# SS2D scan layer: dt*x copied into PSUM by ScalarE instead of TensorE, and products with C made for two tiles at a time

## The chip, the cores and the metric

The kernel runs on one core of a Trainium2 chip. The time is the device time of one execution in microseconds, from the first to the last instruction of that core. Before the change it is 18467.62 us, the median of three runs (18457.31 to 18490.28). The execution that the profiler recorded has a span of 18479.8 us.

## What is computed

Four layers work on a batch of eight images of 56 x 56 pixels with 128 channels. Layers 0, 2 and 3 are deformable convolutions and are not touched. Layer 1 is a visual state-space block ("SS2D"): after a projection, a 3 x 3 convolution and SiLU, each image is read as a sequence of L = 3136 positions in K = 4 directions, and each direction runs a linear recurrence with 256 channels and N = 16 states for each channel. This is the part of the reference that the change bears on:

```python
dt = jax.nn.softplus(dt + dt_projs_b[None, :, :, None])
A = -jnp.exp(A_logs).reshape(K, Di, N)

def step(h, t):
    dt_t, u_t, B_t, C_t = t
    h = h * jnp.exp(dt_t[..., None] * A) + (dt_t * u_t)[..., None] * B_t[:, :, None, :]
    y = jnp.einsum('bkdn,bkn->bkd', h, C_t)
    return (h, y)
```

Each channel and state has a decay exp(dt * A), an input dt * x * B, a recurrence over the positions, and an output that is the sum over the 16 states of h * C.

## The kernel before

**Tiles.** A direction of an image is cut into four chunks of 784 positions (SC). Eight images, four directions and four chunks make 128 steps, which run one after the other. Within a step there are 256 x 16 rows of (channel, state); one tile holds 32 channels with 4 states each on 128 partitions, by 784 positions. So a step has 32 tiles: eight channel groups (`cg`) by four state groups (`sg`), with `sg` running fastest. "Group" below means the four tiles of one `cg`.

**What a tile does.** `decay` (L1346) has ScalarE write dA = exp(dt * A) into PSUM (two buffers). `inputs` makes u = dt * x * B: for the first three tiles of a group VectorE multiplies (L1356) dt * x, which it reads in PSUM, with B; for the fourth GpSimd does it (L1352, tile `up`, one buffer), from SBUF. The dt * x of a group gets into PSUM through `spread` (L1340): TensorE multiplies it with the identity, two matmuls for each group, which the trace shows as four records, into the tile `dtu`. `dtu` has one buffer of two banks, so the next group's can be written only when VectorE has made the third u of this group. Then VectorE runs the recurrence (L1449, a scan) into `h` (three buffers), ScalarE copies its last column to `st` for the next chunk (L1452, a tiny instruction), GpSimd multiplies h with C into `hc` (L1454, six buffers), and TensorE sums the states by matmuls with a 0/1 matrix into `acc` (`add_sums`, L1378). `close_sums` (L1389) has ScalarE copy `acc` out once every eight tiles, and `open_sums` (L1370) starts the next one.

**Around it.** `prepare` (L1241 on) makes dt, dt * x, B and C of the next step in pieces, with matmuls into the one `misc` bank, ScalarE activations (L1265 to L1269) and two GpSimd operations on `dd` (L1271, L1273) for each half of the channels. The input stage of the next image and the output stage of finished chunks run in the background, a piece every tile or two. The SyncE queue issues all transfers: `fetch_dt` (L1291) for a group, two groups ahead, and `fetch_row` (L1284) for B and C of the next step, four rows of each, in five buffers each.

**What sets the order.** The whole layer is written out without a loop. A scheduler puts the instructions of each engine into one fixed order when the program is built; on the chip each engine takes its instructions in that order, and an instruction that has to wait holds up all that stand behind it on its engine. `add_sums` is traced under `issue_after(self.last_spread)`, which puts its matmuls behind the last `spread` on TensorE.

Of the kernel before, what the change touches and what calls it, by code (L numbers as in the profile page):

```python
# [41 lines left out]
F32 = mybir.dt.float32  # L42
# [76 lines left out]
SC, SR = 784, 14  # L119
NSC = L // SC  # L120
SH = SC // 2
# [11 lines left out]
TC, TS = 32, 4  # L133
NCG, NSG = DI // TC, NST // TS
# [855 lines left out]
class Vss:  # L990
# [286 lines left out]

    def fetch_row(self, s, x, sg):

        name = "bc"[x]  # L1280
        t = s[name, sg] = self.work.tile([128, SC], F32, name=name, tag=name, bufs=NSG + 1)
        r = s["rows"]
        src = bass.AP(tensor=r.tensor, offset=r.offset + TS * sg * 2 * SC + x * SC, ap=[[0, TC], [2 * SC, TS], [1, SC]])
        self.nc.sync.dma_start(out=t, in_=src)  # L1284
# [15 lines left out]
    def scans(self):  # L1300
        nc, w = self.nc, self.w
        self.gates, self.sums = {}, {}
        self.y = self.img.tile([128, NCH, L], F32, name="y", tag="y")
        steps = [(i, k, c) for i in range(self.images) for k in (1, 3, 0, 2) for c in (range(NSC) if k < 2 else reversed(range(NSC)))]

        order = [(cg, sg) for cg in range(NCG) for sg in range(NSG)]
# [5 lines left out]
        state = [dict() for _ in steps]  # L1312
# [9 lines left out]
        def advance(count):  # L1322
            for _ in range(count):
                while tasks:
                    try:
                        next(tasks[0])
                        break
                    except StopIteration:
                        tasks.popleft()

        def on_pool(t):

            return order[t][1] == NSG - 1

        def spread(at, t):

            s, (cg, sg) = state[at], order[t]
            ps = s["dtu", cg] = self.pdtu.tile([128, 2, 512], F32, name="dtu", tag="dtu")
            for b in range(2):
                last = nc.tensor.matmul(ps[:, b, :SH], lhsT=self.net.ident, rhs=s["dt", cg][:, 1, SH * b : SH * (b + 1)], start=True, stop=True)  # L1340
            self.last_spread = last.ins

        def decay(at, t):
            (i, k, c), s, (cg, sg) = steps[at], state[at], order[t]
            da = s["dA", t] = self.pda.tile([128, 1024], F32, name="dA", tag="dA")
            nc.scalar.activation(da[:, :SC], s["dt", cg][:, 0], AF.Exp, scale=w["A"][:, k, NSG * cg + sg : NSG * cg + sg + 1])  # L1346

        def inputs(at, t):
            s, (cg, sg) = state[at], order[t]
            if on_pool(t):  # L1350
                u = self.work.tile([128, SC], F32, name="up", tag="up", bufs=1)
                nc.gpsimd.tensor_mul(u, s["dt", cg][:, 1], s["b", sg])  # L1352
            else:
                u = self.work.tile([128, SC], F32, name="u", tag="u", bufs=2)
                halves = [v.rearrange("p (x e) -> p x e", x=2) for v in (u, s["b", sg])]
                nc.vector.tensor_mul(halves[0], s["dtu", cg][:, :, :SH], halves[1])  # L1356
            s["u", t] = u
# [13 lines left out]

        def add_sums(at, group):
            acc = state[at]["acc"]
            with self.tc.issue_after(self.last_spread):
                for (cg, sg), hc in group:
                    for b in range(2):
                        r = 64 * b + TC * (cg % 2)
                        nc.tensor.matmul(acc[r : r + TC, :SH], lhsT=w["sum"], rhs=hc[:, SH * b : SH * (b + 1)], start=False, stop=sg == NSG - 1)  # L1378

        def close_sums(at, t):  # L1380
            (i, k, c), acc, (h, r) = steps[at], state[at]["acc"], place(t)
# [12 lines left out]
            if t == NT - 1:  # L1394
                state[at] = None
                if k == 2:
                    tasks.extend(self.output_stage(i, e) for e in (2 * c + 1, 2 * c))

        spread(*units[0])
        decay(*units[0])  # L1400
        inputs(*units[0])
        st = ready = None
        group, late = [], deque()
        zeros = self.zeros()
        for now, (at, t) in enumerate(units):
            (i, k, c), s, (cg, sg) = steps[at], state[at], order[t]
            forward = k < 2
            if t == 0:
                if at % NSC == 0:
                    st = self.prep.tile([128, NT], F32, name="st", tag="st", bufs=2)  # L1410
                    nc.gpsimd.memset(st, 0.0)
                if at % (NDIR * NSC) == 0 and i + 1 < self.images:
                    tasks.append(self.input_stage(i + 1))
                ready = iter(())
                if at + 1 < len(steps):
                    if steps[at + 1][0] > i:
                        self.load_xb(i + 1)
                    ready = self.prepare(state[at + 1], *steps[at + 1][1:])
            if t % (2 * NSG) == 0:
                late.append((now + 5, open_sums, (at, t)))  # L1420
            while late and late[0][0] <= now:
                _, do, args = late.popleft()
                do(*args)
            if t % 2 == 0:
                next(ready, None)

            if sg == 1:
                to = divmod(NCG * at + cg + 2, NCG)
                if to[0] < len(steps):
                    self.fetch_dt(state[to[0]], to[1])  # L1430
            if t in (3, 19):
                next(zeros, None)

            for x, when in enumerate(((25, 28, 29, 30), (26, 29, 30, 31))):
                if t in when and at + 1 < len(steps):
                    self.fetch_row(state[at + 1], x, when.index(t))
            if now + 1 < len(units):
                decay(*units[now + 1])
                if not on_pool(units[now + 1][1]):
                    inputs(*units[now + 1])  # L1440

                if sg == NSG - 3 and now + 3 < len(units):
                    spread(*units[now + 3])
            if now + 2 < len(units) and on_pool(units[now + 2][1]):
                inputs(*units[now + 2])
            hh = self.work.tile([128, SC], F32, name="h", tag="h", bufs=3)
            step = 1 if forward else -1
            u, dA = s.pop(("u", t)), s.pop(("dA", t))
            nc.vector.tensor_tensor_scan(hh[:, ::step], dA[:, :SC][:, ::step], u[:, ::step], st[:, t : t + 1], ALU.mult, ALU.add)  # L1449
            if c != (NSC - 1 if forward else 0):  # L1450
                last = SC - 1 if forward else 0
                nc.scalar.copy(st[:, t : t + 1], hh[:, last : last + 1])  # L1452
            hc = self.work.tile([128, SC], F32, name="hc", tag="hc", bufs=6)
            nc.gpsimd.tensor_mul(hc, hh, s["c", sg])  # L1454
            group.append((order[t], hc))
            if t % 2:
                late.append((now + 3, add_sums, (at, group)))
                group = []
                if t % (2 * NSG) == 2 * NSG - 1:
                    late.append((now + 5, close_sums, (at, t)))  # L1460
            if t % 2 or t % 4 == 0 or (i == self.images - 1 and k == 2):
                advance(1)
# [81 lines left out]
```

## Time and profile before

The scan layer lies between 2366 us and 13800 us of the span: the first scan starts at 2365.9 us, the last ends just before 13801 us. The other layers lie before and after it. The table is of the profiled execution.

| | before |
|---|---|
| median of three runs | 18467.62 us |
| span of the profiled execution | 18479.8 us |
| the scan layer, from 2366 to 13800 us | 11434 us |
| one step (a 128th of it) | 89.3 us |
| VectorE busy in the scan layer | 10264 us |
| GpSimd busy in the scan layer | 10454 us |
| ScalarE busy in the scan layer | 7052 us |
| TensorE (matmul) busy in the scan layer | 8638 us |

A row of the profile's groups of instructions names the line, the engine, the operation, output and inputs, then how often it ran, its total busy time in us and the mean of one in ns, and then the idle time of its engine just before it, with what ended that idle time. A list of waits names for one engine which instruction waited for which, with the sum, the count and the longest in us. A line of the timeline has the start and the length in us; an "x4" is four records run together, and the bracket is the idle time before them.

### The profile page before, as it was taken

How to read it: one execution, taken by the hardware profiler on the slowest of the kernel's cores; microseconds unless marked ns; L12 is line 12 of the kernel's file. 1: busy time of each engine (PE TensorE's matmuls, PEld its weight loads, DVE VectorE, ACT ScalarE, POOL GpSimd, SP SyncE). 2: the span in 40 equal slices, each digit the busy share in tenths (PEclk: the TensorE clock that was granted, in tenths of full speed). 3: DMA queues.
4: the chain of work that ended last, by engine and by line, in shares of the span. 5: the costliest groups of instructions: out<-in, count | busy, mean ns of one | idle time of the engine just before them, and what ended most of it. 6: DMA issues, size and time to landing. Idle time of an engine off the chain costs nothing. (4 is left out here: it accounts for less than half of the span.)

```text
span 18479.8 us, 257190 instructions
## 1 busy us (share of the span) xinstructions
PE 13780.6 (75%) x89795; PEld 6844.2 (37%) x89795; DVE 15510.8 (84%) x18797; ACT 11145.4 (60%) x20690; POOL 11801.5 (64%) x6462
## 2 busy tenths in 40 slices
PE   5777787678678778678778768767665888577777
PEld 4555422222222222222222222222224666455555
DVE  8888379988988988988988898898985887688886
ACT  4666565566566566566566656656554666456666
POOL 2221089998998998998998998899981111222221
PEclk7878888889889889889888888888886888677777
DMA  7777444444443444344343443443433777577777
GB/s 215 205 210 200 122 158 160 162 158 148 142 149 137 146 147 140 140 150 139 140 150 136 143 152 135 143 150 136 147 122 110 196 198 198 143 204 204 201 204 175
DMA packets 1341779, 2961.90 MB, mean 160 GB/s; under 512 B 91168, under 2 KB 892132, under 8 KB 1325836
## 3 DMA queue, kind: packets, MB, share of 16 engines
q1 hardware_dynamic: 1340460, 2945.21, 51.4%
q8 instruction: 718, 11.76, 0.3%
q14 instruction: 601, 4.92, 0.1%
HBM read 2243.88 MB, written 866.92 MB: 168 GB/s over the span
## 5 line engine op out<-in xcount | busy, mean ns | idle before, releaser
L1454 POOL TENSOR_TENSOR hc<-h,c 128x784 f32<-128x784 f32 x4096 | 7560.9, 1873 | 764.2 <-DVE h L1449 534.4
L1449 DVE TENSOR_TENSOR_SCAN h<-dA,st,u 128x784 f32<-128x784 f32 x3072 | 5569.9, 1838 | 316.2 <-ACT dA L1346 182.3
L1346 ACT ACTIVATE dA<-dt,v_A 128x784 f32<-128x784 f32 x4096 | 3742.8, 915 | 719.1 <-DVE h L1449 717.8
L1356 DVE TENSOR_TENSOR u<-dtu,b 128x784 f32<-128x784 f32 x3072 | 2875.7, 957 | 559.9 <-PE dtu L1340 555.5
L1378 PE MATMUL acc<-hc,v_sum 128*32 128x392 f32 x16384 | 3222.3, 552 | 105.8 <-POOL hc L1454 105.6
L1340 PE MATMUL dtu<-dt,ident 128*128 128x392 f32 x4096 | 2105.1, 642 | 1512.1 <-issue 1102.6
L736 POOL TENSOR_TENSOR ay<-hat,om 112x756 f32<-112x756 f32 (+2 forms) x192 | 525.8, 2738 | 2750.0 <-ACT hat L727 2346.6
L1449 DVE TENSOR_TENSOR_SCAN h<-dA,st,up 128x784 f32<-128x784 f32 x1024 | 1876.7, 1833 | 242.4 <-POOL hc L1454 176.7
L1352 POOL TENSOR_TENSOR up<-dt,b 128x784 f32<-128x784 f32 x1024 | 1900.3, 1856 | 132.1 <-DVE h L1449 110.8
L807 ACT COPY st<-pt 128x448 f32<-128x448 f32 (+1 forms) x2240 | 1177.8, 542 | 1216.4 <-PE pt L805 1210.1
L1452 ACT COPY st<-h 128x1 f32<-128x1 f32 x3072 | 581.7, 189 | 2159.0 <-DVE h L1449 2150.5
L1340 PEld LDWEIGHTS dtu<-dt,ident 128*128 128x128 f32 x4096 | 862.0, 235 | 2564.6 <-issue 1672.2
L775 DVE TENSOR_TENSOR win<-win,patch 112x252 f32 (+2 forms) x3456 | 1695.4, 503 | 124.4 <-DVE win L775 34.2
L805 PE MATMUL pt<-ident,sw 112*128 112x112 f32 (+2 forms) x8960 | 1609.7, 310 | 199.1 <-DMA sw<-skew 198.8
L1378 PEld LDWEIGHTS acc<-hc,v_sum 128*32 128x32 f32 x16384 | 769.8, 117 | 2488.2 <-issue 1675.4
L766 POOL MEMSET win<- 128x1820 f32 (+2 forms) x384 | 630.1, 1646 | 1466.2 <-DMA skew<-win 1159.6
L821 PE MATMUL yps<-st,xw 128*32 128x48 f32 (+5 forms) x35840 | 1077.7, 245 | 397.6 <-ACT st L807 394.8
L805 PEld LDWEIGHTS pt<-ident,sw 112*128 112x128 f32 (+2 forms) x8960 | 1119.5, 161 | 485.6 <-DMA sw<-skew 166.9
L772 DVE TENSOR_TENSOR patch<-ay,hat 112x756 f32<-112x756 f32 (+2 forms) x1152 | 1221.3, 1066 | 22.5 <-POOL ay L736 19.5
L821 PEld LDWEIGHTS yps<-st,xw 128*32 128x32 f32 (+2 forms) x35840 | 757.0, 126 | 825.9 <-ACT st L807 476.1
L1112 PE MATMUL misc<-xn,v_tap 128*128 128x448 f32 x2016 | 867.3, 574 | 96.5 <-ACT xn L1146 61.2
L725 ACT ACTIVATE hat<-om,taps 112x252 f32<-112x252 f32 x1280 | 755.7, 729 | 287.1 <-DVE patch L772 273.4
(165 smaller groups left out, 19517.2 us busy)
## 6 DMA issues: line engine op xcount, KB each, us to landing
dt<-dds SPq DMA_DIRECT2D x1024, 784.0 KB
b<-rows SPq DMA_DIRECT2D x512, 392.0 KB
c<-rows SPq DMA_DIRECT2D x512, 392.0 KB
dds<-dd SPq DMA_DIRECT2D x256, 784.0 KB
sw<-skew SPq DMA_DIRECT2D x224, 812.0 KB
sw<-skew SPq DMA_DIRECT2D x224, 672.0 KB
sw<-skew SPq DMA_DIRECT2D x224, 588.0 KB
xw<-table SPq DMA_DIRECT2D x224, 320.0 KB
```

The source lines that it names most:

```text
L772: nc.vector.tensor_mul(patch[:n], bcast(a, 3, KX), bcast(b, 2, KY))
L775: self.last_add = nc.vector.tensor_add(to, to, patch[:n, NCB * p : NCB * (p + 1)]).ins
L805: last = nc.tensor.transpose(ps[:m, n * g : n * (g + 1)], sw[:n, g, p : p + m], self.net.ident[:n, :n])
L807: nc.scalar.copy(st[:m], ps[:m, : G * n])
L821: self.nc.tensor.matmul(yps[CG * g : CG * (g + 1), t0:t1], lhsT=xw[:m, k + part, CG * g : CG * (g + 1)], rhs=st[:m, at + t0 : at + t1], st ...
L1340: last = nc.tensor.matmul(ps[:, b, :SH], lhsT=self.net.ident, rhs=s["dt", cg][:, 1, SH * b : SH * (b + 1)], start=True, stop=True)
L1346: nc.scalar.activation(da[:, :SC], s["dt", cg][:, 0], AF.Exp, scale=w["A"][:, k, NSG * cg + sg : NSG * cg + sg + 1])
L1352: nc.gpsimd.tensor_mul(u, s["dt", cg][:, 1], s["b", sg])
L1356: nc.vector.tensor_mul(halves[0], s["dtu", cg][:, :, :SH], halves[1])
L1378: nc.tensor.matmul(acc[r : r + TC, :SH], lhsT=w["sum"], rhs=hc[:, SH * b : SH * (b + 1)], start=False, stop=sg == NSG - 1)
L1449: nc.vector.tensor_tensor_scan(hh[:, ::step], dA[:, :SC][:, ::step], u[:, ::step], st[:, t : t + 1], ALU.mult, ALU.add)
L1454: nc.gpsimd.tensor_mul(hc, hh, s["c", sg])
```

## The change

Three edits go together. `spread` is a copy by ScalarE, SBUF to PSUM, in place of two matmuls by TensorE, and `add_sums` no longer stands behind the last `spread`. The tiles h, hc and C hold two tiles side by side (`h` two such pairs, `hc` three, `c` three), and GpSimd multiplies a pair in one instruction of 1568 elements for each partition; the scans still run one for each tile. The rows of C are fetched at tiles 26, 28, 31 and 31 in place of 26, 29, 30 and 31. The program is built with `dynamic_dma_scratch_size=8192`, half of what the ring for DMA descriptors had before.

```diff
     def fetch_row(self, s, x, sg):
-        name = "bc"[x]
-        t = s[name, sg] = self.work.tile([128, SC], F32, name=name, tag=name, bufs=NSG + 1)
+        if x == 0:
+            t = s["b", sg] = self.work.tile([128, SC], F32, name="b", tag="b", bufs=NSG + 1)
+        else:
+            if sg % 2 == 0:
+                s["c", sg // 2] = self.work.tile([128, 2, SC], F32, name="c", tag="c", bufs=NSG // 2 + 1)
+            t = s["c", sg // 2][:, sg % 2]
...
             ps = s["dtu", cg] = self.pdtu.tile([128, 2, 512], F32, name="dtu", tag="dtu")
-            for b in range(2):
-                last = nc.tensor.matmul(ps[:, b, :SH], lhsT=self.net.ident, rhs=s["dt", cg][:, 1, SH * b : SH * (b + 1)], start=True, stop=True)
-            self.last_spread = last.ins
+            nc.scalar.copy(ps[:, :, :SH], s["dt", cg][:, 1].rearrange("p (b e) -> p b e", b=2))
...
         def add_sums(at, group):
             acc = state[at]["acc"]
-            with self.tc.issue_after(self.last_spread):
-                for (cg, sg), hc in group:
...
+            for (cg, sg), hc in group:
...
-            for x, when in enumerate(((25, 28, 29, 30), (26, 29, 30, 31))):
+            for x, when in enumerate(((25, 28, 29, 30), (26, 28, 31, 31))):
...
-            hh = self.work.tile([128, SC], F32, name="h", tag="h", bufs=3)
+            if t % 2 == 0:
+                pair = self.work.tile([128, 2, SC], F32, name="h", tag="h", bufs=2)
+            hh = pair[:, t % 2]
...
-            hc = self.work.tile([128, SC], F32, name="hc", tag="hc", bufs=6)
-            nc.gpsimd.tensor_mul(hc, hh, s["c", sg])
-            group.append((order[t], hc))
             if t % 2:
-                late.append((now + 3, add_sums, (at, group)))
-                group = []
+                hc = self.work.tile([128, 2, SC], F32, name="hc", tag="hc", bufs=3)
+                nc.gpsimd.tensor_mul(hc, pair, s["c", sg // 2])
+                late.append((now + 3, add_sums, (at, [(order[t - 1], hc[:, 0]), (order[t], hc[:, 1])])))
...
-    nc = bacc.Bacc("TRN2", target_bir_lowering=False, num_devices=1)
+    nc = bacc.Bacc("TRN2", target_bir_lowering=False, num_devices=1, dynamic_dma_scratch_size=8192)
```

More of the change, by code (lines that the diff above doesn't have):

```diff
@@ L1373, in add_sums @@
             acc = state[at]["acc"]
-            with self.tc.issue_after(self.last_spread):
-                for (cg, sg), hc in group:
-                    for b in range(2):
-                        r = 64 * b + TC * (cg % 2)
-                        nc.tensor.matmul(acc[r : r + TC, :SH], lhsT=w["sum"], rhs=hc[:, SH * b : SH * (b + 1)], start=False, stop=sg == NSG - 1)
+            for (cg, sg), hc in group:
+                for b in range(2):
+                    r = 64 * b + TC * (cg % 2)
+                    nc.tensor.matmul(acc[r : r + TC, :SH], lhsT=w["sum"], rhs=hc[:, SH * b : SH * (b + 1)], start=False, stop=sg == NSG - 1)
         def close_sums(at, t):
@@ L1402, in scans @@
         st = ready = None
-        group, late = [], deque()
+        late = deque()
         zeros = self.zeros()
@@ L1432, in scans @@
                 next(zeros, None)
-            for x, when in enumerate(((25, 28, 29, 30), (26, 29, 30, 31))):
-                if t in when and at + 1 < len(steps):
-                    self.fetch_row(state[at + 1], x, when.index(t))
+            for x, when in enumerate(((25, 28, 29, 30), (26, 28, 31, 31))):
+                for row in range(NSG):
+                    if t == when[row] and at + 1 < len(steps):
+                        self.fetch_row(state[at + 1], x, row)
             if now + 1 < len(units):
```

## The prediction, made before the changed kernel ran

> **What bounds the kernel now.** First the busy time of each engine by stage, since only the scan layer is changed. The columns are the stretch, its length, and for each engine its busy time and (x) its number of instructions; then the clock granted to TensorE and the DMA share.
>
> ```profile
> core 0: us, PE busy (x) PEld busy (x) DVE busy (x) ACT busy (x) POOL busy (x), PEclk, DMA share, GB/s
> 2366.00:13800.00 11434.00, 8637.61 (x31300) 3030.12 (x31298) 10264.15 (x8600) 7051.73 (x13027) 10453.60 (x5761) 0.86 0.41 145
> ```
>
> VectorE and GpSimd are both busy for nine tenths of these 11434 us. Neither is the bound alone: they pass tiles to each other and each waits for the other at times. VectorE's work (10264 us) does not change, so the layer's time after is 10264 us plus what VectorE waits. It waits 11434 - 10264 = 1170 us now. What for, is told by its list of waits in this stretch (sum in us, times, longest):
>
> ```profile
> DVE u L1356 <- PE dtu L1340: 473.5, 258, 7.8
> DVE h L1449 <- ACT dA L1346: 234.3, 199, 4.2
> DVE h L1449 <- POOL hc L1454: 214.4, 165, 3.2
> DVE h L1449 <- POOL up L1352: 3.8, 5, 1.8
> ```
>
> The reader should see that the largest wait is for the matmuls which the change takes away, (the group's row below books 555 us for it; I use the smaller figure), and that next come ScalarE's decay and GpSimd's product, both of which it touches. What is left over, 1170 - 473 - 234 - 218 = 245 us, is mostly background pieces (statistics that wait for matmuls or loads). Third, the costs, from the groups of instructions (count | busy us, mean ns | idle before):
>
> ```profile
> L1454 POOL TENSOR_TENSOR hc<-h,c 128x784 f32<-128x784 f32 x4096 | 7560.9, 1873 | 764.2 <-DVE h L1449 534.4
> L1449 DVE TENSOR_TENSOR_SCAN h<-dA,st,u 128x784 f32<-128x784 f32 x3072 | 5569.9, 1838 | 316.2 <-ACT dA L1346 182.3
> L1346 ACT ACTIVATE dA<-dt,v_A 128x784 f32<-128x784 f32 x4096 | 3742.8, 915 | 719.1 <-DVE h L1449 717.8
> L1356 DVE TENSOR_TENSOR u<-dtu,b 128x784 f32<-128x784 f32 x3072 | 2875.7, 957 | 559.9 <-PE dtu L1340 555.5
> L1340 PE MATMUL dtu<-dt,ident 128*128 128x392 f32 x4096 | 2105.1, 642 | 1512.1 <-issue 1102.6
> L1352 POOL TENSOR_TENSOR up<-dt,b 128x784 f32<-128x784 f32 x1024 | 1900.3, 1856 | 132.1 <-DVE h L1449 110.8
> L1268 ACT ACTIVATE sp<-sp 128x784 f32<-128x784 f32 x256 | 218.9, 855 | 0.1
> ```
>
> Last, a stretch of the timeline shows how the largest wait comes about:
>
> ```profile
> 7022.73 0.95 DVE L1356 TENSOR_TENSOR u<-dtu,b 128x784 f32<-128x784 f32 x1
> 7023.78 2.95 PE L1340 MATMUL dtu<-dt,ident 128*128 128x392 f32 x4 [2.98 <-issue]
> 7023.86 1.83 DVE L1449 TENSOR_TENSOR_SCAN h<-dA,st,u 128x784 f32<-128x784 f32 x1
> 7026.77 0.97 DVE L1356 TENSOR_TENSOR u<-dtu,b 128x784 f32<-128x784 f32 x1 [0.63 <-PE dtu L1340]
> ```
>
> TensorE stands idle until VectorE has made the third u and freed `dtu`; its four records then take 2.95 us (at other places 1.58 us), and VectorE, which in this order has only one scan and some statistics in between, sits for 0.63 us.
>
> **Part 1, dt * x by ScalarE.** TensorE loses 4096 records, 2105 us. ScalarE gains 1024 copies of 128x784 from SBUF to PSUM, which no row shows. Nearest from above is `sp` (L1268), the same size with no operand for each partition: 855 ns. From below, copies of 128x448 take 530 ns at L1120 and those of 64x392 479 ns at L1389: 51 ns for 56 elements, 0.91 ns each, so 530 + 336 x 0.91 = 836 ns; `sp` and the 448 copy give (855 - 530) / 336 = 0.97 ns each. I take 0.84 us, between 0.80 and 0.90. ScalarE's load is then 7052 + 1024 x 0.84 = 7912 us, 71% of a layer of some 11100 us: not a bound by its sum, only by lateness.
>
> Is the copy there in time? It may start when the third u is done. In the rebuilt order of the changed kernel, VectorE has two scans between the third u and the next group's first u in 680 of 1023 groups: 3.67 us for 0.84 us of copy. In 342 groups it has one, 1.84 us, as in the timeline above. ScalarE in that time also has one state copy (0.19 us) and one decay (0.915 us) before it at the worst: 1.95 us against 1.84 us, 0.1 us late, and usually the decay was done during the third u. So the wait for `dtu` does not vanish altogether; longer ones come where `prepare` or a background stage puts five or more ScalarE instructions in front. Laying the durations of the rows along the rebuilt order of ScalarE, I find some 33 of 1023 copies late, by 1 us each. With as much again for what a count on paper leaves out, 60 us are left of 473 (ends: 20, if ScalarE is never late, and 250, half of now). **Gain 413 us.**
>
> What it costs elsewhere: a copy that stands in front of a decay delays it by 0.84 us, and a decay has little room, since it needs the scan two tiles earlier to have freed its PSUM buffer. The same count gives 120 decays late in the old order and 256 in the new, 59 us and 138 us in sum. Against it stands that ScalarE now waits 1280 us for matmuls (`acc`, `misc`; ten rows of its list of waits added), each time with decays queued behind, and TensorE has 2105 us less in its queue. I put the decay wait at 300 us after 234 (ends: 150, and 450 if the count's 79 us more comes out threefold). **Loss 66 us.**
>
> [...] By the row, 8638 - 2102 = 6536 us remain. [...]
>
> **Part 2, products in pairs.** GpSimd had 4096 products, busy 7560.9 us, so 1.846 us each where they follow each other (the mean record is 1.873). Now 2048 of twice the size. By the row alone, nothing fixed to save, a pair takes 2 x 1.846 = 3.69 us. GpSimd's memsets (1334 ns for 1484 elements, 1990 ns for 2268) have 0.837 ns an element and 92 ns fixed; with that, 2 x 1.873 - 0.09 = 3.65 us. [...] I take 3.55 us: GpSimd's work falls by 2048 x (3.69 - 3.55) = 290 us to 10160 us (ends: 0 and 370).
>
> Against that, a pair starts only when both scans are done. Take one group of VectorE, 3 x 0.957 + 4 x 1.837 = 10.22 us. The first pair is ready at 5.6 us and must be multiplied before the next group's first scan at 12.1 us: 6.5 us for 3.55 us of work, 3.0 us to spare. Before, tile 0 was ready at 3.7 us and its buffer wanted again by tile 3's scan at 8.4 us: 4.6 us for 1.85, 2.8 us to spare. So the pair, with four tiles of h in place of three, is not tighter. GpSimd's work for a group is 2 x 3.55 + 1.86 = 8.96 us, 1.26 us less than VectorE's (9.24 and 0.98 before); that is how fast it catches up after the two `dd` operations, 1.86 + 2.05 = 3.9 us, twice a step. They overrun the 3.0 us by about 0.9 us unless GpSimd was ahead. But VectorE, no longer held by `dtu`, will press harder on it. I leave the wait for products at 200 us after 218 (ends 100 and 450). The wait of GpSimd for `acc` (176 us) should shrink with a freer TensorE; it is not VectorE's and counts nothing here.
>
> **Part 3, the rest.** C's second pair is asked for at tile 31 and waits on SyncE for the product of tiles 28 and 29; behind it stands a dt fetch two groups ahead. Needed by the second product of the next step, a group later, it has some 10 us for 2 x 392 KB, at the layer's 145 GB/s 5.5 us. Free; if not, 128 steps pay. The smaller descriptor room costs nothing: the profile shows only hardware queues. The other layers keep their instructions.
>
> **Sum.** VectorE waits 60 + 300 + 200 + 245 = 805 us after 1170: 365 us less, and the span is 18480 - 365 = 18115 us. The median lies 12 us below the profiled span: **18103 us**, 2.0% faster.
>
> **Rivals.**
> *ScalarE late, slower.* If the copy starts only after the state copy of the third scan, then in the 640 groups where the next u follows that scan directly, VectorE waits 0.19 + 0.84 + some 0.05 = 1.08 us: 691 us in place of 60, so 18734 us. It decides from a mean wait of (365 + 60) / 1024 = 0.42 us for each copy on. For it: ScalarE already waits 2150 us for scans at L1452, in order. Against: the rebuilt order has nearly all copies ahead of that state copy.
> *GpSimd takes the wait over, no change.* GpSimd is busier than VectorE today; if the pair saves nothing (3.69 us), what `dtu` gives up returns as waits for products: 218 + 350 us, so 18471 us. Against: its 980 us of idle time, 645 us of it waiting for scans.
> [...]
> *Cold TensorE.* At a clock near 0.6, `acc` and `misc` come late and ScalarE's 1280 us of waits grow by half; were two thirds of that passed on to VectorE, the gain is gone with 60 us more: 18530 us.
>
> **How the numbers follow.** Forecast 0.54, more gained 0.13, GpSimd 0.13, ScalarE late 0.13, cold TensorE 0.07. The forecast's own range is 17950 to 18350 us (its ends not all at once). With parts of the rivals the range is 17880 to 18600 us. A change below 0.2%, 37 us, can't be told from none. Faster: 0.54 + 0.13 + a third of GpSimd's case = 0.71; same 0.07, the middle of that case; slower 0.22.
>
> **What would show it.** Right: VectorE's wait for `dtu` under 100 us, now named after ScalarE; a pair near 3.55 us; the layer near 11070 us. Wrong: waits for `dtu` or decays above 600 us together (ScalarE), a pair at 3.69 us with waits for products above 450 us (GpSimd), or a granted clock below 0.65 with ScalarE's waits for matmuls above 1900 us.

## The result: slower, 19336.6 us, and the profile after

The changed kernel takes 19336.58 us in the median (19328.48 to 19354.06), 1.0466 times the kernel before, with a 95% interval of 1.0453 to 1.0479 (the kernel before, now with a fourth run, has a median of 18471.8 us). The forecast was 18103 us, 2.0% faster. The busy time by engine in the scan layer of the changed kernel (same columns as before: length, TensorE, weight loads, VectorE, ScalarE, GpSimd, clock, DMA share, GB/s):

```profile
2361.00:14678.00 12317.00, 8209.97 (x27214) 2469.39 (x27214) 10266.01 (x8601) 7743.75 (x14052) 10182.90 (x3716) 0.77 0.39 135
```

The layer has grown from 11434 to 12317 us. Only ScalarE has more work than before (7744 us after 7052); VectorE is busy for 10266 us as ever, GpSimd for 271 us less. VectorE's busy time being the same, the growth is in its waits. VectorE's list, then ScalarE's:

```profile
DVE h L1453 <- ACT dA L1348: 1204.5, 517, 7.3
DVE u L1358 <- ACT dtu L1343: 283.9, 126, 5.9
DVE h L1453 <- POOL hc L1459: 168.2, 136, 4.4
```

```profile
ACT y L1390 <- PE acc L1379: 795.7, 204, 8.6
...
ACT out L1390 <- PE acc L1379: 358.6, 81, 7.3
ACT dbl L1253 <- PE misc L1251: 344.1, 148, 6.3
ACT sp L1265 <- PE misc L1264: 340.3, 246, 8.1
```

For comparison, ScalarE's waits at the copies of `acc` in the kernel before:

```profile
ACT y L1389 <- PE acc L1378: 402.0, 237, 7.4
...
ACT out L1389 <- PE acc L1378: 132.5, 73, 4.4
```

VectorE waits 1204 us for decays, after 234. It was not the decays' own cost (914 ns each, 915 before): ScalarE stands 1154 us at its copies of `acc`, after 535, and longer at the readers of `misc`. All its waits for matmuls together are 2416 us after 1284. One step further back stands TensorE. Its waits for products at the sums, in the kernel before and then in the changed one:

```profile
PE acc L1378 <- POOL hc L1454: 105.2, 123, 2.0
```

```profile
PE acc L1379 <- POOL hc L1459: 2539.7, 1062, 7.4
```

The three operations that the change touched, from the groups of instructions by form:

```profile
L1459 POOL TENSOR_TENSOR hc<-h,c 128x1568 f32<-128x1568 f32 x2048 | 7265.3, 3551 | 1885.2 <-DVE h L1453 1531.1 <-issue 142.8 <-PE acc L1379 119.1
...
L1379 PE MATMUL acc<-hc,v_sum 128*32 128x392 f32 x16384 | 4404.7, 653 | 2548.1 <-POOL hc L1459 2539.7 <-POOL st L1412 6.1
...
L1343 ACT COPY dtu<-dt 128x784 f32<-128x784 f32 x1024 | 829.2, 810 | 36.2 <-DVE u L1358 35.6
```

A pair costs 3551 ns and a copy 810 ns, near the 3.55 and 0.84 us of the forecast. GpSimd now stands idle for 1531 us before its products, waiting for scans. How the ring of waits closes is seen in one stretch of the changed kernel's timeline:

```profile
7017.35 1.84 DVE L1453 TENSOR_TENSOR_SCAN h<-dA,st,up 128x784 f32<-128x784 f32 x1
7018.21 1.86 POOL L1271 TENSOR_TENSOR dd<-dd,sp 128x784 f32<-128x784 f32 x1
...
7019.33 0.91 ACT L1348 ACTIVATE dA<-dt,v_A 128x784 f32<-128x784 f32 x1
...
7020.15 2.23 POOL L1273 TENSOR_TENSOR dd<-dd,xb 128x784 f32<-128x784 f32 x1
7022.34 3.49 POOL L1459 TENSOR_TENSOR hc<-h,c 128x1568 f32<-128x1568 f32 x1
...
7025.89 2.83 PE L1379 MATMUL acc<-hc,v_sum 128*32 128x392 f32 x8 [5.33 <-POOL hc L1459]
...
7028.76 0.88 ACT L1390 COPY y<-acc 64x392 f32<-64x392 f32 x1 [8.52 <-PE acc L1379]
...
7029.50 0.91 ACT L1348 ACTIVATE dA<-dt,v_A 128x784 f32<-128x784 f32 x1
...
7030.50 1.85 DVE L1453 TENSOR_TENSOR_SCAN h<-dA,st,u 128x784 f32<-128x784 f32 x1 [5.67 <-ACT dA L1348]
```

Read it from below. The scan waits 5.67 us for a decay. That decay waited for nothing of its own: it stands in ScalarE's queue behind the copy of `acc`, which ScalarE had reached at 7020.2 us and at which it stood for 8.52 us. The copy waits for the block's last sums, these for the last pair's product. That product started 3.15 us after its second scan had ended (7019.19 us), because GpSimd had the two `dd` operations first; it then took 3.49 us, and the sums 2.83 us. While VectorE stands, no new tile reaches GpSimd, which in turn waits 4.66 us for a scan before its product at 7035.74 us; so the lost time is not caught up.

### The profile page after: what moved, and what is told of

Its sections match the earlier page's. It is cut to its first block, busy times and chain, and to the rows that moved or that the text cites. A ratio compares the mean times of both kernels' runs of the same rounds, so it can differ in the third digit from the quotient of the medians.

```text
span 19352.5 us, 244401 instructions
## 1 busy us (share of the span) xinstructions
PE 13356.4 (69%) x85699; PEld 6290.5 (33%) x85699; DVE 15516.2 (80%) x18797; ACT 11837.6 (61%) x21714; POOL 11535.1 (60%) x4414
## 5 line engine op out<-in xcount | busy, mean ns | idle before, releaser
L1459 POOL TENSOR_TENSOR hc<-h,c 128x1568 f32<-128x1568 f32 x2048 | 7265.3, 3551 | 1885.2 <-DVE h L1453 1531.1
L1379 PE MATMUL acc<-hc,v_sum 128*32 128x392 f32 x16384 | 4404.7, 653 | 2548.1 <-POOL hc L1459 2539.7
L1379 PEld LDWEIGHTS acc<-hc,v_sum 128*32 128x32 f32 x16384 | 967.6, 130 | 5806.4 <-POOL hc L1459 3704.4
L1390 ACT COPY y<-acc 64x392 f32<-64x392 f32 x768 | 575.9, 750 | 803.6 <-PE acc L1379 795.7
L1372 PE MATMUL acc<-y,ident 128*64 128x392 f32 x1536 | 597.2, 777 | 570.6 <-ACT y L1390 348.4
```

Source lines behind the costliest of these rows:

```text
L1459: nc.gpsimd.tensor_mul(hc, pair, s["c", sg // 2])
```

## The experiments

First the fixed order of the instructions; the built program has it before any run, and the counts here are of the traced executions. For each copy of `acc` in ScalarE's order, count which tile's decay stands next behind it, from the last tile of the block that the copy closes. The smaller the number, the sooner a late product stops the scans. Each block of eight tiles has two copies, and all blocks but the last, which no decay follows, are counted.

| kernel | the sums stand behind | 3 | 4 | 5 | 6 | 7 or more |
|---|---|---|---|---|---|---|
| before | the spread | 0 | 2 | 52 | 564 | 404 |
| changed | nothing | 348 | 135 | 83 | 436 | 20 |
| `free_sums_only` | nothing | 658 | 35 | 101 | 172 | 56 |
| `after_sums` | the copy of dt * x | 0 | 28 | 229 | 693 | 72 |

The last two rows are runs that come below. In the changed kernel 483 of 1022 copies stand 3 or 4 tiles behind their block, where 2 did before. The sums themselves have lost their slack: from the end of a pair's (second) product to the start of its sums on TensorE, the median in the traces is 5.6 us before and 0.06 us in the changed kernel. Before, TensorE did its waiting at the spread (1512 us idle in the prediction's row), and when the spread was through, the products behind it were mostly there.

The first four runs part the change along this. `copy_only` has ScalarE's copy without the pairs (and the sums free, as there is no matmul of the spread to stand behind); `pairs_only` has the pairs, with TensorE's spread and the order as before; `free_sums_only` is the kernel before with nothing but the order edge dropped; `after_anchored` is the changed kernel with the copies of `acc` put back.

```diff
 free_sums_only, against the kernel before
-            with self.tc.issue_after(self.last_spread):
-                for (cg, sg), hc in group:
...
+            for (cg, sg), hc in group:
...
 after_anchored, against the changed kernel
-            nc.scalar.activation(da[:, :SC], s["dt", cg][:, 0], AF.Exp, ...
+            self.last_decay = nc.scalar.activation(da[:, :SC], s["dt", cg][:, 0], AF.Exp, ...
...
-                nc.scalar.copy(to, acc[64 * b : 64 * (b + 1), :SH] if k == 2 else ...
+                with self.tc.issue_after(self.last_decay.ins):
+                    nc.scalar.copy(to, acc[64 * b : 64 * (b + 1), :SH] if k == 2 else ...
```

> Only ScalarE's copy of dt*x, with the sums no longer held behind it; products and buffers single as before. Four theories of the 880 us that the change lost. EARLY COPIES (without the order to stand behind the spread, the scheduler puts the sums' matmuls and with them ScalarE's copies of acc earlier in the fixed order; the chip's GpSimd is later than the order assumes, so ScalarE stands at the acc copy with decays behind it): in the rebuilt order 317 of 650 acc copies here stand 3 or 4 tiles behind the end of their block, as in the changed kernel and unlike before (6 or 7), so slower than before, 18800 to 19300 us, decay wait 600 to 1100 us. SCALARE LOAD (850 us more of work on it): as slow as the changed kernel, 19200 to 19400 us. LATE PAIRS: no slower than before, 18100 to 18500 us. COLD TENSORE: granted clock 0.77 and 19000 us or more.

> Only the pairs (h, hc, C, fetch times, descriptor ring as in the changed kernel); dt*x spread by TensorE and the sums held behind it, as before. EARLY COPIES: acc copies stand 6 or 7 tiles behind their block in the rebuilt order, so no loss: 18300 to 18600 us, decay wait under 350 us. SCALARE LOAD: as before, 18350 to 18500 us. LATE PAIRS: the whole loss is here, 19100 to 19400 us, with TensorE waiting some 2500 us for products. COLD TENSORE: as before, clock 0.86.

> The kernel before with one edit: the sums' matmuls no longer stand behind the last spread; TensorE still spreads, products single. EARLY COPIES: the rebuilt order has 400 of 629 acc copies 3 or 4 tiles behind their block, so slower than before although no engine has more work: 18800 to 19300 us. SCALARE LOAD, LATE PAIRS and COLD TENSORE: none of their causes is here, 18300 to 18600 us.

> The changed kernel with one edit: ScalarE's copies of acc stand behind the last decay emitted before them, which puts all of them 6 or 7 tiles behind their block in the rebuilt order (3 to 6 in the changed kernel). EARLY COPIES: most of the loss comes back, 18200 to 18700 us, decay wait under 500 us. SCALARE LOAD, COLD TENSORE: little changes, 19100 to 19400 us. LATE PAIRS: some of it, 18900 to 19300 us, since the products are as late as before.

| run | us | ratio to before | 95% interval |
|---|---|---|---|
| copy_only | 18708.3 | 1.0117 | 1.0101 to 1.0134 |
| pairs_only | 18526.0 | 1.0021 | 1.0013 to 1.0029 |
| free_sums_only | 19391.1 | 1.0489 | 1.0472 to 1.0507 |
| after_anchored | 18704.6 | 1.0113 | 1.0096 to 1.0129 |

The ratios are to runs of the kernel before in the same set, whose medians are 18493.7, 18474.5 and 18488.4 us for the three sets; a difference of some 20 us between runs of different sets says nothing.

The dropped edge alone, with not one instruction more or fewer, costs as much as the whole change. The pairs alone, with the edge kept, cost 0.2%. ScalarE's copy alone, although its sums are free, costs 1.2%. So neither the load on ScalarE nor the pairs make the loss by themselves, and a cold TensorE is not needed for it: the clock of the span in `free_sums_only` was 0.82, as before (0.83). Three expectations were missed in size: `copy_only` was faster and `free_sums_only` slower than the 18800 to 19300 us of EARLY COPIES, and `after_anchored` lies just above 18200 to 18700 us. What the lost edge costs depends on what stands behind the sums. The first theory was only half right. In `free_sums_only` VectorE lost its time at the spread and not at decays; its waits and TensorE's:

```profile
DVE u L1356 <- PE dtu L1340: 1354.7, 638, 9.2
DVE h L1448 <- ACT dA L1346: 335.7, 247, 4.7
...
PE acc L1377 <- POOL hc L1453: 1852.4, 1330, 6.9
```

The reader sees that it is one place on TensorE, sums that stand at the head of its queue before their product is made, and that whoever stands behind them pays: there the spread's own matmuls. And `after_anchored` kept a decay wait of 660 us, where under 500 were expected: with its copies of `acc` moved out of the way (they wait 7 us in all), ScalarE stands at other readers of TensorE's results:

```profile
ACT sp L1265 <- PE misc L1264: 666.2, 255, 8.1
...
ACT dbl L1253 <- PE misc L1251: 351.4, 146, 8.0
```

So the second theory: not ScalarE's copies, but the sums' own place on TensorE. The next four runs put them back behind the copy of dt * x that has replaced the spread, by an edge that only the scheduler sees.

```diff
 after_sums, against the changed kernel (copy_sums: the same two edits in copy_only)
-            nc.scalar.copy(ps[:, :, :SH], s["dt", cg][:, 1].rearrange("p (b e) -> p b e", b=2))
+            self.last_spread = nc.scalar.copy(ps[:, :, :SH], s["dt", cg][:, 1].rearrange("p (b e) -> p b e", b=2)).ins
...
-                    nc.tensor.matmul(acc[r : r + TC, :SH], lhsT=w["sum"], rhs=hc[...], start=False, stop=sg == NSG - 1)
+                    m = nc.tensor.matmul(acc[r : r + TC, :SH], lhsT=w["sum"], rhs=hc[...], start=False, stop=sg == NSG - 1)
+                    self.tc.add_manual_dep(m.ins, self.last_spread.name, mybir.DependencyInfo(mybir.DependencyClass.NoSync, mybir.DependencyReason.DATA), reason="sums")
```

> The changed kernel with one edit: the sums' matmuls are placed behind the last copy of dt*x (an edge for the scheduler, no wait on the chip), as they stood behind the spread before. In the rebuilt order the acc copies stand 5 or 6 tiles behind their block (3 to 6 in the changed kernel, 6 or 7 before) and the readers of misc 5 to 7 tiles behind the last product that TensorE must have summed (3 to 5 in the changed kernel). ORDER OF THE SUMS (all of the loss comes from TensorE meeting the sums too early, and with it everything queued behind): 18000 to 18400 us, faster than before, decay wait under 350 us, TensorE's wait for products under 800 us. COPIES OF ACC ALONE (the order matters only through ScalarE's acc copies): no better than with those moved, 18650 to 18800 us. SCALARE LOAD plus COLD TENSORE (the 1.1% that was left after the acc copies were moved): 18650 to 18800 us, clock 0.76 to 0.78.

> The same with the acc copies behind the decay as well (6 or 7 tiles). ORDER OF THE SUMS: within 100 us of the one without, 18000 to 18400 us. COPIES OF ACC ALONE: 18650 to 18800 us. SCALARE LOAD plus COLD TENSORE: 18650 to 18800 us.

> The kernel before with ScalarE's copy of dt*x, products single, and the sums' matmuls placed behind that copy. ORDER OF THE SUMS: 18100 to 18450 us, no slower than before, since the wait for dtu falls from 473 us to under 150 us and nothing else is late; that this was 18708 us with the sums free would be the order alone. SCALARE LOAD plus COLD TENSORE: 18650 to 18800 us, as without the edge.

> The same with the acc copies behind the decay as well. ORDER OF THE SUMS: within 100 us of the one without. SCALARE LOAD plus COLD TENSORE: 18650 to 18800 us. Against the run with pairs it shows what pairs bring once the order is right: by the pair's 3.55 us in place of 3.69 us on GpSimd 50 to 150 us, or nothing if GpSimd does not bind.

| run | us | ratio to before | 95% interval |
|---|---|---|---|
| after_sums | 18331.3 | 0.9924 | 0.9907 to 0.9940 |
| after_both | 18316.1 | 0.9913 | 0.9896 to 0.9930 |
| copy_sums | 18226.9 | 0.9868 | 0.9852 to 0.9885 |
| copy_both | 18238.7 | 0.9872 | 0.9856 to 0.9889 |

One edge takes the changed kernel from 19337 to 18331 us: from 4.7% slower than before to 0.8% faster. The edge places the sums and, with them, whatever the scheduler puts behind them, so this run shows the edge as the cause and not the share of each follower. Once it is there, moving ScalarE's copies adds nothing. Two expectations for waits in `after_sums` were missed: VectorE waited 446 us for decays and TensorE 1455 us for products, where under 350 and 800 were expected; the last set bears on that. In `copy_sums`, which has no pairs, VectorE's waits are close to what was forecast for the full change:

```profile
DVE h L1447 <- ACT dA L1344: 344.7, 214, 5.5
DVE h L1447 <- POOL hc L1452: 178.9, 193, 3.0
DVE u L1354 <- ACT dtu L1339: 83.1, 63, 4.1
```

These eight runs and the changed kernel give a square of four: with the sums behind, single products take 18227 us and pairs 18331 us; with the sums free, 18708 and 19337 us. Pairs thus lose in both rows, 104 and 629 us, although GpSimd's work is less with them, and they lose most where the order is wrong; about half of the changed kernel's loss against `copy_sums` comes only when both meet. The expectation that they would bring 50 to 150 us was a miss. The last four runs ask why, measure the clock, test the acc copies with single products, and try a fourth buffer of h.

```diff
 sums_split, against after_sums
-            if t % 2:
+            if t % 2 == 0:
                 hc = self.work.tile([128, 2, SC], F32, name="hc", tag="hc", bufs=3)
-                nc.gpsimd.tensor_mul(hc, pair, s["c", sg // 2])
+            nc.gpsimd.tensor_mul(hc[:, t % 2], hh, s["c", sg // 2][:, t % 2])
+            if t % 2:
...
 after_warm, against the changed kernel
+            for b in range(2):
+                r = 64 * b + TC * (group[0][0][0] % 2)
+                nc.tensor.matmul(acc[r : r + TC, :SH], lhsT=w["none"], rhs=w["fc1"][:, :SH], start=False, stop=False)
...
 copy_only_anchored, against copy_only: the edit of after_anchored
...
 copy_sums_h4, against copy_sums
-            hh = self.work.tile([128, SC], F32, name="h", tag="h", bufs=3)
+            hh = self.work.tile([128, SC], F32, name="h", tag="h", bufs=4)
...
-    nc = bacc.Bacc("TRN2", target_bir_lowering=False, num_devices=1)
+    nc = bacc.Bacc("TRN2", target_bir_lowering=False, num_devices=1, dynamic_dma_scratch_size=8192)
```

> The changed kernel with the sums behind the copy of dt*x (18331 us), and GpSimd again makes one product for each tile as soon as its scan is done; pair buffers, C's fetch times and the descriptor ring stay as in the changed kernel. Why are pairs 104 us slower than single products (18227 us) with the right order? LATE PRODUCT (a pair's first half waits for the second scan, so TensorE and the acc copy get it later): this falls to 18180 to 18260 us, TensorE's wait for products from 1455 to under 950 us. BUFFERS OR FETCHES (two pair buffers of h are freed later than three single ones, or C comes later): it stays at 18310 to 18370 us.

> The changed kernel, with two more matmuls before the sums of each pair, which add zero times a weight to acc and wait for no product: they only keep TensorE busy (some 1500 us of added work, free of waits). COLD TENSORE (half a clock makes the sums 2.83 us in place of 1.51 us and so the loop through acc longer): clock up from 0.77 to 0.85 or more and 18900 to 19200 us. ORDER ALONE: 19300 us or more, whatever the clock does, since more work stands on the engine that is late.

> ScalarE's copy of dt*x with single products and the sums free (18708 us), with only the acc copies moved behind the decay. COPIES OF ACC ALONE: as fast as with the sums moved, 18200 to 18300 us. MATMULS BEHIND THE SUMS (the background matmuls of misc stand behind sums that wait for products, and ScalarE stands at their readers): only a part comes back, 18400 to 18600 us.

> The fastest kernel so far (copy of dt*x by ScalarE, single products, sums behind the copy, 18227 us) with four buffers of h in place of three, in the space that the halved descriptor ring leaves. If VectorE's 179 us of waits for products are for free buffers of h: 18080 to 18180 us. If GpSimd's work itself binds there, at 10427 of 11180 us, or the halved ring costs something: 18200 to 18300 us.

| run | us | ratio to before | 95% interval |
|---|---|---|---|
| sums_split | 18131.6 | 0.9807 | 0.9793 to 0.9820 |
| after_warm | 19479.2 | 1.0540 | 1.0524 to 1.0557 |
| copy_only_anchored | 18430.3 | 0.9972 | 0.9960 to 0.9984 |
| copy_sums_h4 | 18135.3 | 0.9810 | 0.9796 to 0.9823 |

*Late product.* `sums_split` keeps the pair buffers, C's fetch times and the halved ring, and only makes each product as soon as its scan is done. It is 200 us faster than `after_sums`, more than expected. TensorE's wait for products, in `after_sums` and then in `sums_split`:

```profile
PE acc L1379 <- POOL hc L1460: 1454.6, 673, 6.4
```

```profile
PE acc L1379 <- POOL hc L1460: 897.3, 746, 5.4
```

So joining the two products costs some 200 us. TensorE's shorter wait is what a late first half explains; VectorE's wait for decays falls too, from 446 to 376 us, and GpSimd's own for scans from 723 to 325 us. How much of the time goes by which path was not separated.

A fourth buffer of h is a gain: `copy_sums_h4`, which differs from `copy_sums` by it and the halved ring, takes 18135 us in place of 18227 us. VectorE's wait for products falls from 179 us to this:

```profile
DVE h L1447 <- POOL hc L1452: 27.9, 25, 3.0
```

`sums_split`, with two pair buffers of h and three of C, reaches the same 18132 us, but there this wait stays at 190 us; what makes up its gain over `copy_sums` was not separated.

*Cold TensorE.* The added matmuls raised the clock of the span from 0.766 to 0.809 and shortened the sums (653 ns before), but took 2196 us themselves:

```profile
L1384 PE MATMUL acc<-hc,v_sum 128*32 128x392 f32 x16384 | 4002.6, 591 | 2056.4 <-POOL hc L1464 2050.1 <-POOL st L1417 3.1
...
L1380 PE MATMUL acc<-v_fc,v_none 128*32 128x392 f32 x8192 | 2195.9, 580 | 0.0
```

In the scan layer the clock came to 0.83, where 0.85 or more was expected. The time rose by 143 us. The warmer clock with that much ballast did not help here; whether a warm clock for nothing would, this run can't tell. That the clock is not what was lost follows from `copy_sums` and `sums_split`, faster than before at 0.78.

*Copies of acc with single products.* Moving them wins 278 us of the 481 us that separate `copy_only` from `copy_sums`. They are part of the loss. For the rest the background matmuls behind the sums are the likely cause: ScalarE waits 1073 us at the readers of `misc` here and 593 us in `copy_sums`. No run moved those alone.

## Why the prediction was wrong

*What VectorE waits decides, since its work does not change*: right. Its busy time stayed at 10266 us, and the layer's growth is its waits, 2051 us where 805 were forecast: 284 for `dtu` (60), 1204 for decays (300), 206 for products (200) and 357 for the rest (245).

*The wait for dtu, 473 to 60 us*: the wait was 284 us in the changed kernel, 68 in `after_sums` and 83 in `copy_sums`. The copy at 0.84 us was 0.81. With the order right, the gain that was forecast is there.

*The decay's wait, 300 us*: this is the term that failed, with 1204 us. The step behind it read: "Against it stands that ScalarE now waits 1280 us for matmuls [...] each time with decays queued behind, and TensorE has 2105 us less in its queue." It took a lighter TensorE for a sooner TensorE. The waits at matmuls went from 1284 to 2416 us, because the sums stand further forward in TensorE's order and wait there for products, 2540 us after 105. The count of late decays (256, 138 us) laid the durations of the rows along the rebuilt order of ScalarE, and durations hold no waits for TensorE. There was a sign of that: the same count gave 59 us for the kernel before, where 234 us were measured. The rebuilt order had the answer in it: the table of copies could have been made before the run. And the dropped `issue_after` was in the diff; the prediction never priced it.

*Pairs at 3.55 us*: measured 3.551. The rows gave 3.69 us with nothing saved and 3.65 us with the memsets' 92 ns. Nothing in them showed less, so 3.55 us was the author's estimate, and that it came out to the nanosecond is luck; the other runs with joined products have 3.54 to 3.57 us. For the 0.13 of "more gained" and the 17880 us at which the wide range begins, no run shows anything: the fastest took 18132 us. GpSimd's work fell by 271 us where 290 were said. That this was worth nothing is the surprise: the argument weighed only when h must be free again (200 us forecast, 206 found) and not when TensorE gets the product.

*Rivals.* "ScalarE late" had the right side and named the engine that VectorE waits for, and its sign came (waits for `dtu` and decays above 600 us together: 1488 us). But it put 691 us on waits for `dtu`, behind the state copy of the third scan, where 284 us were measured (68 and 83 us with the order right), and its 18734 us are less than a third of the loss. "GpSimd takes the wait over" is not seen. "Cold TensorE" named the engine behind it, and half of its sign came: ScalarE's waits for matmuls were above 1900 us (2416 us), but the clock not below 0.65. It was 0.77. TensorE was busy for 8210 us and not for the 6536 us that the rows left it, since each record of the sums took 653 ns after 552. What sets the clock was not shown. In the layer it was 0.85 to 0.87 in the three kernels in which TensorE spreads (busy for 76 to 77% of the layer), 0.75 to 0.80 in the ten with ScalarE's copy and no added matmuls (67 to 70%), and 0.83 in `after_warm` (72%); the faster `copy_sums`, `copy_both`, `sums_split` and `copy_sums_h4` are at 0.78 to 0.79.

*The rest.* The transfers and the halved ring do no harm that these runs show: `sums_split` and `copy_sums_h4` have the ring, `sums_split` C's new fetch times too, and both are the fastest.

## What to carry to other kernels

When an operation moves to another engine, carry over the edges that hung on it: an order edge is part of the schedule, and its loss here cost 4.9% by itself, and putting it back in the changed kernel won 5.2%. In a fixed order, price for each engine not only its load but what its queue's head waits for, and who stands behind. An engine that waits early in its queue may be what keeps later work from stopping others (before, TensorE stood 1512 us at the spread and 105 us at the sums; with the edge dropped alone, 1852 us at the sums): look for the sums, copies and readers that have come nearer to their producers. Joining two products saved 0.14 us of 3.69 here and delayed the first half's consumers (18132 to 18331 us); one more buffer of h was worth more (18227 to 18135 us).

## What the hardware showed that was not expected

Two products joined saved 0.14 us of 3.69, and the joining cost 200 us all the same (18132 to 18331 us). TensorE's granted clock in the scan layer was 0.86 before, at a busy share of 76%, and 0.77 in the changed kernel, at 67%. Eight records of the sums took 1.51 us in a stretch with a granted clock of 1.00 (7012.90 to 7014.60 us of the changed kernel) and 2.83 us in one with 0.50 (7025.89 to 7028.72 us); about 2.83 us took 670 of 1901 such eights in the changed kernel and 119 of 1987 before. What was not expected is how little this decided: the two fastest kernels of the study, `sums_split` and `copy_sums_h4`, run at a clock of 0.78 over the span and 1.9% under the time before.
